# Edge lists of a graph layer: rows of keys gathered by their number, a written order on three engines, packed comparisons, norms loaded as rows

## The chip, the core and the metric

The kernel runs on one core of a Trainium2 chip. The metric is the device time of one execution in microseconds (us), lower being better; the time before is the median of three executions. One more execution was recorded by the hardware profiler, and all durations below come from it.

A core has TensorE (PE in the profile, with its weight loads as PEld), VectorE (DVE), ScalarE (ACT), GpSimd (POOL) and SyncE (SP). Each works through its own instructions in order. SP, ACT and POOL also issue transfers.

## What is computed

The input is a table x of 1250 rows of 768 numbers and an edge list of 41250 pairs (src, dst), sorted by dst. Reduced to what matters:

```python
def gat_layer(x, W, a_src, a_dst, b, src, dst):     # twice, relu between
    h = x @ W
    e = leaky_relu((h @ a_src)[src] + (h @ a_dst)[dst], 0.2)
    w = exp(e - segment_max(e, dst)[dst])
    alpha = w / segment_sum(w, dst)[dst]
    return segment_sum(h[src] * alpha[:, None], dst) + b

x = x + gat_layer(relu(gat_layer(layernorm(x), ...)), ...)
y = layernorm(x)
y = y + attention(layernorm(y, ln1_g, ln1_b))       # 12 heads of 64
y = y + moe(layernorm(y, ln2_g, ln2_b))             # 8 experts, the best 2 of each row
return x + y
```

Everything is float32.

## The kernel before

**The plan.** The 1250 nodes are ten tiles of 125 rows (T = 125, NT = 10). The graph layer isn't done edge by edge. The kernel first turns the edge list into a dense table `cnt`: how many edges lead from each source node to each target node. Then attention over edges is dense work on 1250 x 1250 tables, and the sum over edges is a matrix product with h. Everything up to the finished `cnt` is the first stage, and it is what the change is about. It ends near 144 us; the two graph layers, attention, routing and the experts follow.

**Keys and windows.** Each edge becomes a key, dst * 1250 + src. The keys, 330 to a row and 125 rows, lie in SBUF as `key` and are stored to DRAM as `keys`. For each node the kernel finds the position of its first edge, and a gather (an indirect DMA issued by GpSimd) fetches 64 keys from there: the node's window. To find the position, the kernel before makes a 0/1 table `within` (125 rows x 1250 nodes: does this node's first edge lie in this row?) from the first key of a row (`head`) and the first key of the next (`after`, from the small loads `rn`). For each tile, a matmul with `within` as weights fetches the one row of keys that belongs to each node (`pk`, L263), and VectorE counts the keys in it that are smaller than the node's own first possible key (L264) and adds the row's first edge number (L266). When all ten tiles are done, ten gathers follow (L275), and each window has the node's base subtracted (L305) to become `win`.

**Comparisons.** The windows, in which each entry is a source node's number or a mark for none, are transposed into `lt` and split into a tile number `jb` and a place within the tile `pb`. There are 625 pairs of nodes, taken in 25 groups of 25 (NP = 625, PG = 25). For each group VectorE compares pb with `lane` to make `oh` (L349, 128 x 128 x 25 in bfloat16); for every five groups it compares jb with `upto`, the numbers 1 to 20, to make `ohj` (L346). TensorE then takes one matmul for each pair (L353): oh's 128 columns as weights, 20 columns of ohj as the moving operand. ScalarE copies the counts into `cnt` (L357). `oh` has two buffers.

**Beside it.** The same stage normalises the ten tiles of x (statistics and `ln_stats` on VectorE, the root and the scaling on ScalarE at L123 and L298), transposes them into xnT (L136, copied out at L285), projects the first three tiles with W (L186, `EARLY` = 3), multiplies W by the two attention vectors (L169, `attention_vectors`; `rep` holds a vector copied to all partitions) and multiplies xnT by the results (L177, `attention_terms`, three chunks of six matmuls, copied out as `er`). A float32 matmul shows in the profile as two passes.

**Order.** A scheduler places the instructions on each engine. The programmer's order is one of its inputs and isn't kept. A loop over `turns` stands ready for lists that do not fit the windows; it makes no pass on these inputs. The four norm vectors, `lnp`, are loaded one number to a partition (L495), and the router's weights `wr` after them (L496); both are wanted only in the second graph layer and later, but the scheduler has put these loads at the beginning, on ACT's queue.

Of the kernel before, what the change touches and what calls it, by code (L numbers as in the profile page):

```python
# [10 lines left out]
F32 = mybir.dt.float32  # L11
F16 = mybir.dt.float16
BF16 = mybir.dt.bfloat16
# [14 lines left out]
def gnn_ffn_kernel(  # L28
# [24 lines left out]
    nc = tc.nc  # L53
# [62 lines left out]
    def ln_stats(row):  # L116
        st = small.tile([T, 2, 6], F32, tag="st", name="st")
        for s in range(2):
            nc.vector.bn_stats(st[:, s, :], row[:, s * DH:(s + 1) * DH])
        mv = small.tile([T, 2], F32, tag="mv", name="mv")  # L120
        nc.vector.bn_aggr(mv, st.rearrange("p a b -> p (a b)"))
        sd = small.tile([T, 1], F32, tag="sd", name="sd")
        nc.scalar.activation(sd, mv[:, 1:2], AF.Sqrt, bias=eps[:T])  # L123
        rstd = small.tile([T, 1], F32, tag="rstd", name="rstd")
        nc.vector.reciprocal(rstd, sd)
        return mv[:, 0:1], rstd
# [29 lines left out]
    with tc.tile_pool(name="cnt", bufs=1) as cpool:  # L156
# [6 lines left out]
        def attention_vectors(layer, w, a_src, a_dst, pool):  # L163
            for i, a in enumerate((a_src, a_dst)):
                rep = pool.tile([P, D], F32, tag="rep", name="rep", bufs=1)
                nc.scalar.dma_start(rep, bass.AP(tensor=a.tensor, offset=a.offset, ap=[[0, P], [1, D]]))
                for c in range(DC):
                    scr = pool.tile([P, D], F32, tag="scr", name="scr", bufs=1)
                    nc.vector.scalar_tensor_tensor(scr, w[:, c, :], 1.0, rep, op0=ALU.mult, op1=ALU.mult,  # L169
                                                   accum_out=wa[:, layer, c, i:i + 1])  # L170

        def attention_terms(layer, xT, psum):

            for c0, w in CHUNKS:
# [4 lines left out]
                nc.scalar.copy(er[:, c0:c0 + w], pe[0:2, :w])  # L179
# [16 lines left out]
        EARLY = 3  # L196
        with tc.tile_pool(name="edge", bufs=1) as ep, \
# [6 lines left out]
            rn = ep.tile([T, 2], I32, name="rn")  # L204
            nc.gpsimd.memset(rn, 2 * N)
            for i, (eng, a) in enumerate(((nc.sync, dst), (nc.scalar, src))):
                eng.dma_start(ri[:, i, :], a.rearrange("(p e) -> p e", p=T))
                with nc.allow_non_contiguous_dma(reason="one edge of each row"):
                    eng.dma_start(rn[0:T - 1, i:i + 1], a[EC:E].rearrange("(p e) -> p e", p=T - 1)[:, 0:1])
            xrows = []  # L210
            for t in range(4):
# [4 lines left out]
            rf = ep.tile([T, 2, EC], F32, name="rf")  # L216
            nc.vector.tensor_copy(rf, ri)
            key = ep.tile([T, EC + 1], F32, name="key")
            nc.vector.scalar_tensor_tensor(key[:, :EC], rf[:, 0, :], float(N), rf[:, 1, :],
                                           op0=ALU.mult, op1=ALU.add)  # L220
# [3 lines left out]
            nc.sync.dma_start(keys[0:E].rearrange("(p e) -> p e", p=T), key[:, :EC])  # L224
            nc.gpsimd.iota(key[:, EC:EC + 1], pattern=[[0, 1]], base=0, channel_multiplier=EC,
                           allow_small_or_imprecise_dtypes=True)
            after = ep.tile([T, 2], F32, name="after")
            nc.vector.tensor_copy(after, rn)
            nc.vector.scalar_tensor_tensor(after[:, 0:1], after[:, 0:1], float(N), after[:, 1:2],
                                           op0=ALU.mult, op1=ALU.add)  # L230
# [17 lines left out]
            upto = ep.tile([P, 2 * NT], BF16, name="upto")  # L248
            nc.gpsimd.iota(upto, pattern=[[1, 2 * NT]], base=1, channel_multiplier=0,
# [6 lines left out]
            within = ep.tile([T, N], F32, name="within")  # L256
            nc.vector.tensor_scalar(within, nodes, head, None, ALU.is_gt)
            nc.vector.scalar_tensor_tensor(within, nodes, after[:, 0:1], within, op0=ALU.is_le, op1=ALU.mult)
            junk = ep.tile([T, EC], F32, name="junk")
            place = ep.tile([T, NT], F32, name="place")  # L260
            for t in range(NT):
                pk = gpt.tile([P, 4, P], F32, tag="tr", name="pk").rearrange("p a b -> p (a b)")
                nc.tensor.matmul(pk[:T, :EC + 1], within[:, t * T:(t + 1) * T], key, start=True, stop=True)  # L263
                nc.vector.scalar_tensor_tensor(junk, pk[:T, :EC], node[:, t:t + 1], ones[:T, :],  # L264
                                               op0=ALU.is_lt, op1=ALU.mult, accum_out=place[:, t:t + 1])
                nc.vector.tensor_tensor(place[:, t:t + 1], place[:, t:t + 1], pk[:T, EC:EC + 1], ALU.add)  # L266
            nc.vector.tensor_scalar(place, place, 0.0, float(E), ALU.max, ALU.min)
            at = ep.tile([T, NT], I32, name="at0")
            begun = nc.vector.tensor_copy(at, place)

            win = ep.tile([T, NT, SL], F32, name="win")
            kws = []
            for t in range(NT):
                kw = op.tile([T, SL], F32, tag="kw", name="kw", bufs=NT)
                nc.gpsimd.indirect_dma_start(  # L275
                    out=kw, out_offset=None, in_=keys.rearrange("(e o) -> e o", o=1),
                    in_offset=bass.IndirectOffsetOnAxis(ap=at[:, t:t + 1], axis=0))
                kws.append(kw)
# [10 lines left out]
            for t in range(NT):  # L289
                if t < len(xrows):  # L290
                    xn = xrows[t]
                else:
                    xn = op.tile([T, D], F32, tag="xn", name="xn", bufs=4)
                    split_rows(nc.sync if t % 2 == 0 else nc.scalar, xn, x[t * T:(t + 1) * T, :])
                mean, rstd = ln_stats(xn)
# [711 lines left out]
```

## Time and profile before

| | |
|---|---|
| median of three executions | 1547.34 us (1546.9 to 1551.69) |
| the profiled execution | 1548.87 us; span from first to last instruction 1546.8 us |
| TensorE busy | 1458.0 us (94%), 5990 matmul passes |
| VectorE busy | 804.2 us (52%) |
| ScalarE busy | 597.5 us (39%) |
| GpSimd busy | 417.9 us (27%) |
| mean granted TensorE clock | 0.968 |
| first pass of L263, L353; last end of L353 | 22.27, 81.61 and 143.77 us |

A line of the order of time has the start, the length, the engine, the line of the kernel, the operation, what is written and read with its shape, how often, and in brackets how long the engine had been idle and what ended that. A line of a group has the number of instructions, then busy time in us and the mean in ns, then the idle time before them and its cause. A table by stretch has, for each engine, the busy time and the number of instructions, then the granted TensorE clock, the share of the DMA engines' time and GB/s.

### The profile page before, as it was taken

The numbers are of one execution on the slowest core, as the hardware profiler recorded it, in microseconds if no ns is written. First come the engines' busy times: TensorE is split into PE (matmuls) and PEld (weight loads), VectorE is DVE, ScalarE is ACT, GpSimd is POOL, SyncE is SP. The second block draws the span as 40 slices with busy tenths as digits, with TensorE's granted clock in tenths as the row PEclk, the third lists the DMA queues.
The fourth block names the chain that finished last, engine by engine and source line by source line (L and its number), as shares of the span: only waits on it lengthen the run. The fifth ranks groups of instructions, "written<-read, shape, count | busy, mean of one in ns | idle before, by whom it ended". The sixth has DMA issues, their size and how long they took to land.

```text
span 1546.8 us, 15957 instructions
## 1 busy us (share of the span) xinstructions
PE 1458.0 (94%) x5990; PEld 783.7 (51%) x5990; DVE 804.2 (52%) x1296; ACT 597.5 (39%) x949; POOL 417.9 (27%) x279
## 2 busy tenths in 40 slices
PE   4797999999999999999999999999988997899997
PEld 2466655554555555553434334334333565456664
DVE  5588643205315651016877877877889665111111
ACT  2422413202413631115665665665666354221211
POOL 3200000000000002004565565675676322122222
PEclk9975999999999999999999999999999998899999
DMA  5201020000021117951000000000030333854643
GB/s 148 56 1 34 8 72 0 1 2 9 0 72 53 57 50 278 406 196 61 1 21 1 22 0 21 1 21 1 1 100 1 111 120 124 302 167 171 229 143 139
DMA packets 50912, 123.83 MB, mean 80 GB/s; under 512 B 8542, under 2 KB 25045, under 8 KB 50833
## 3 DMA queue, kind: packets, MB, share of 16 engines
q1 hardware_dynamic: 30798, 55.21, 10.6%
q0 software_dynamic: 11408, 55.44, 9.5%
q10 hardware_dynamic: 8626, 12.15, 2.8%
q8 instruction: 48, 0.79, 0.2%
q14 instruction: 32, 0.25, 0.1%
HBM read 69.65 MB, written 57.60 MB: 82 GB/s over the span
## 4 chain that ended last, share of the span: by engine, by line
PE 65%; DVE 8%; issue 8%; DMA 4%; ACT 4%; POOL 1%; POOLq 0%; SPq 0%; DVEq 0%; ACTq 0%
PE pagg L465 12%; PE st L592 8%; PE ph L186 8%; PE pav L636 7%; PE pk L555 5%; PE pv L571 5%; PE phe L921 4%; PE pq L555 4%; PE poe L930 4%; DVE sT L622 2%; DMA xd<-yn,slot 2%; PE po L779 2%; ACT sT L595 1%; DMA out_dram<-sofar,ids 1%; DVE most L601 1%
## 5 line engine op out<-in xcount | busy, mean ns | idle before, releaser
L628 POOL TENSOR_TENSOR acc<-acc,sT 125x834 f32<-125x834 f32 (+1 forms) x139 | 272.9, 1963 | 10.9
L465 PE MATMUL pagg<-h,wt 125*125 125x385 f32 (+1 forms) x800 | 262.7, 486 | 0.4 <-DVE wt L458 0.4
L601 DVE TENSOR_TENSOR most<-most,st 125x834 f32<-125x834 f32 (+1 forms) x144 | 146.9, 1020 | 105.1 <-ACT sT L595 101.7
L465 PEld LDWEIGHTS pagg<-h,wt 125*125 125x125 f32 x800 | 147.4, 187 | 106.0 <-DVE wt L458 2.7
L622 DVE TENSOR_TENSOR sT<-sT,mb 125x834 f32<-125x834 f32 (+1 forms) x180 | 174.1, 1015 | 22.6 <-PE mb L617 22.6
L623 ACT ACTIVATE sT<-sT 125x834 f32<-125x834 f32 (+1 forms) x180 | 158.4, 900 | 49.2 <-DVE sT L622 48.9
L595 ACT COPY sT<-st 125x834 f32<-125x834 f32 (+1 forms) x180 | 151.5, 848 | 51.3 <-PE st L592 48.3
L592 PE MATMUL st<-qk 64*125 64x417 f32 (+1 forms) x720 | 164.6, 557 | 3.8 <-DVE most L601 3.8
L636 PE MATMUL pav<-sT,v 125*64 125x417 f32 (+1 forms) x720 | 150.8, 531 | 9.1 <-ACT sT L623 9.1
L533 POOL MEMSET zero<- 128x772 f32 x1 | 0.7, 741 | 538.9 <-PE ptr L136 538.9
L628 POOL TENSOR_TENSOR acc<-sT 125x834 f32<-125x834 f32 (+1 forms) x18 | 35.3, 1962 | 275.3 <-ACT sT L623 275.3
L592 PEld LDWEIGHTS st<-qk 64*125 64x125 f32 x720 | 56.6, 184 | 99.0 <-issue 42.7
L636 PEld LDWEIGHTS pav<-sT,v 125*64 125x64 f32 x720 | 42.5, 136 | 105.7 <-issue 43.9
L930 PE MATMUL poe<-we,hT 128*128 128x384 f32 x264 | 88.8, 486 | 0.0
L555 PE MATMUL pq<-yT,wqk 128*128 128x417 f32 (+1 forms) x216 | 88.1, 534 | 0.0
L779 PE MATMUL po<-wp,aT 128*125 128x384 f32 x240 | 87.5, 498 | 0.0
L921 PE MATMUL phe<-xT,we 128*128 128x384 f32 (+1 forms) x288 | 86.6, 460 | 0.0
L934 DVE SCALAR_TENSOR_TENSOR sofar<-poe,weight,sofar 128x768 f32<-128x768 f32 x25 | 25.4, 1018 | 115.2 <-PE poe L930 115.1
L555 PE MATMUL pk<-yT,wqk 128*128 128x417 f32 (+1 forms) x216 | 84.0, 526 | 0.0
L186 PE MATMUL ph<-gw,xnT 128*125 128x384 f32 x240 | 83.9, 505 | 0.0
L571 PE MATMUL pv<-wv,yT 128*125 128x384 f32 x240 | 79.9, 490 | 1.4 <-issue 1.4
L469 DVE RECIPROCAL rz<-pagg 125x1 f32<-125x1 f32 x20 | 3.3, 165 | 148.1 <-PE pagg L465 148.1
(218 smaller groups left out, 1807.7 us busy)
## 6 DMA issues: line engine op xcount, KB each, us to landing
xd<-zero POOLq DMA_DIRECT2D x8, 3860.0 KB
we<-in_L_ffn_W_dram SPq DMA_DIRECT2D x16, 1152.0 KB
xr<-xd SPq DMA_DIRECT2D x25, 386.0 KB
gw<-in_L_gnn_W_dram SPq DMA_DIRECT2D x2, 2304.0 KB
wqk<-in_L_ffn_Wqkv_dram SPq DMA_DIRECT2D x12, 384.0 KB
xres<-in_x_dram SPq DMA_DIRECT2D x10, 375.0 KB
xsd<-xres ACTq DMA_DIRECT2D x10, 375.0 KB
wv<-in_L_ffn_Wqkv_dram SPq DMA_DIRECT2D x1, 2304.0 KB
```

The source lines that it names most:

```text
L186: nc.tensor.matmul(po[:, s, :DH], xT[:, c, t * T:(t + 1) * T], w[:, c, s * DH:(s + 1) * DH], start=(c == 0), stop=(c == DC - 1))
L465: nc.tensor.matmul(po[:, s, :DH + s], ws[j][:, (d - d0) * T:(d - d0 + 1) * T], h[:, j, s * DH:(s + 1) * DH + s], start=(j == 0), stop=(j = ...
L555: nc.tensor.matmul(pq[:, :w], wqk[:, c, i, :], yT[:, c, c0:c0 + w], start=(c == 0), stop=(c == DC - 1))
L571: nc.tensor.matmul(pv[:T, s, :DH], yT[:, c, t * T:(t + 1) * T], wv[:, c, s * DH:(s + 1) * DH], start=(c == 0), stop=(c == DC - 1))
L592: nc.tensor.matmul(st[:T, i, :w], self.qk[r, 1, j * T:(j + 1) * T], self.qk[r, 0, self.c0:self.c0 + w], start=True, stop=True)
L595: nc.scalar.copy(s[:, :, :w], st[:T, :, :w])
L601: nc.vector.tensor_tensor(self.most[:, :, :w], prev[:, :, :w], st[:T, :, :w], ALU.max)
L622: nc.vector.tensor_tensor(s[:, :, :w], s[:, :, :w], self.mb[:T, :, :w], ALU.subtract)
L623: nc.scalar.activation(s[:, :, :w], s[:, :, :w], AF.Exp)
L628: nc.gpsimd.tensor_tensor(self.acc[:, :, :w], prev[:, :, :w], s[:, :, :w], ALU.add)
L636: nc.tensor.matmul(self.pav[r, :w], v[:, j, hd0:hd0 + HD], s[:, i, :w], start=(j == 0), stop=(j == NT - 1))
L930: nc.tensor.matmul(po[:, d, :DH], hT[:, f, s * P:(s + 1) * P], w2[:, f, d * DH:(d + 1) * DH], start=(f == 0), stop=(f == FC - 1))
```

## The change

In words, in the order of the diff:

- Finding a node's first edge: `begun`, one bfloat16 compare of `nodes` with `head`, replaces `within`; ten matmuls with a single column of ones count how many rows begin before each node, which gives the row's number; a gather by that number fetches the row of 330 keys from DRAM (`gather_row`, three buffers), and `first_edges` counts in it and issues the tile's window gather at once, straight into `win`. `rn` and `after` are gone. `keys` is stored from ACT's queue.
- A written order (`manual_schedule`) for TensorE, VectorE and GpSimd covers row numbers, statistics, normalisation, transposes, the three early projections, the attention vectors and twelve of the eighteen terms; a second one for TensorE and VectorE covers the comparisons, with one of the remaining six terms after every fourth group.
- `upto` and `ohj` are laid out so that the 125 pairs of five groups are innermost; `upto` is written out in full, and TensorE reads ohj's 20 columns 125 elements apart.
- The conversion of the edge lists to float32 (`rf`), which only the loop over `turns` reads, comes after the comparisons.
- The norm vectors are loaded as 24 rows of 128 numbers, transposed by TensorE and copied to `lnp`; these loads, `wr` and the attention vectors' loads keep their place in the program on ACT's queue.

The core of the diff:

```diff
-        def attention_vectors(layer, w, a_src, a_dst, pool):
+        def attention_vectors(layer, w, a_src, a_dst, pool, bufs):
+            def load(a):
+                rep = pool.tile([P, D], F32, tag="rep", name="rep", bufs=bufs)
+                tc.keep_in_program_order(nc.scalar.dma_start(rep, ...))
+                return rep
...
-                with nc.allow_non_contiguous_dma(reason="one edge of each row"):
-                    eng.dma_start(rn[0:T - 1, i:i + 1], a[EC:E].rearrange("(p e) -> p e", p=T - 1)[:, 0:1])
...
-            nc.vector.tensor_copy(rf, ri)
-            nc.vector.scalar_tensor_tensor(key[:, :EC], rf[:, 0, :], float(N), rf[:, 1, :], ...)
+            nc.vector.scalar_tensor_tensor(key, ri[:, 0, :], float(N), ri[:, 1, :], op0=ALU.mult, op1=ALU.add)
...
-            nc.sync.dma_start(keys[0:E].rearrange("(p e) -> p e", p=T), key[:, :EC])
+            nc.scalar.dma_start(keys[0:E].rearrange("(p e) -> p e", p=T), key)
...
-            upto = ep.tile([P, 2 * NT], BF16, name="upto")
-            nc.gpsimd.iota(upto, pattern=[[1, 2 * NT]], base=1, channel_multiplier=0,
+            upto = ep.tile([P, 2 * NT, 5 * PG], BF16, name="upto")
+            nc.gpsimd.iota(upto, pattern=[[1, 2 * NT], [0, 5 * PG]], base=1, channel_multiplier=0,
...
-            for t in range(NT):
-                pk = gpt.tile([P, 4, P], F32, tag="tr", name="pk").rearrange("p a b -> p (a b)")
-                nc.tensor.matmul(pk[:T, :EC + 1], within[:, t * T:(t + 1) * T], key, start=True, stop=True)
-                nc.vector.scalar_tensor_tensor(junk, pk[:T, :EC], node[:, t:t + 1], ones[:T, :],
-                                               op0=ALU.is_lt, op1=ALU.mult, accum_out=place[:, t:t + 1])
...
+            def find_rows():
+                nc.vector.tensor_scalar(begun, nodes, head, None, ALU.is_gt)
+                pk = epc.tile([P, 512], F32, tag="pc", name="pk")
+                for t in range(NT):
+                    nc.tensor.matmul(pk[:T, t:t + 1], begun[:, t * T:(t + 1) * T], oneb,
+                                     start=True, stop=True)
+                return pk
+            def gather_row(t):
+                krows[t] = op.tile([T, EC], F32, tag="kr", name="kr", bufs=LEAD)
+                nc.gpsimd.indirect_dma_start(
+                    out=krows[t], out_offset=None, in_=keys[0:E].rearrange("(p e) -> p e", p=T),
+                    in_offset=bass.IndirectOffsetOnAxis(ap=row[:, t:t + 1], axis=0))
+            def first_edges(t):
+                count = small.tile([T, 1], F32, tag="count", name="count")
+                nc.vector.scalar_tensor_tensor(key, krows[t], node[:, t:t + 1], ones[:T, :],
+                                               op0=ALU.is_lt, op1=ALU.mult, accum_out=count)
+                nc.vector.tensor_tensor(at[:, t:t + 1], count, edges[:, t:t + 1], ALU.add)
+                nc.gpsimd.indirect_dma_start(
+                    out=win[:, t, :], out_offset=None, in_=keys.rearrange("(e o) -> e o", o=1),
+                    in_offset=bass.IndirectOffsetOnAxis(ap=at[:, t:t + 1], axis=0))
...
+            def spread(t):
...
+                stats[t] = ln_root(xrows[t])
+            def normal(t):
+                mean, sd = stats.pop(t)
...
+                nc.scalar.activation(xrows[t], xrows[t], AF.Identity, scale=rstd, bias=less)
+            def columns(t):
+                transpose_rows(gpt, xrows[t], evict_to(xT, t))
...
+            with tc.manual_schedule(engines=fixed):
+                pk = find_rows()
+                spread(0)
+                nc.vector.tensor_scalar(row, pk[:T, :NT], -1.0, None, ALU.add)
+                nc.vector.tensor_scalar(edges, pk[:T, :NT], -1.0, float(EC), ALU.add, ALU.mult)
+                for t in range(LEAD):
+                    gather_row(t)
+                for t in range(4):
+                    if t > 0:
+                        spread(t)
+                        normal(t - 1)
+                normal(3)
+                for t in range(4):
+                    columns(t)
+                for t in range(NT):
+                    first_edges(t)
+                    if t + LEAD < NT:
+                        gather_row(t + LEAD)
+                    if t % 3 == 0 and t // 3 < EARLY:
+                        project(xT, gw, h, gpo, [t // 3])
+                    if 0 < t <= 6:
+                        spread(t + 3)
+                    vector(0 if t < 3 else 1 if t < 5 else 2)
+                    if 0 < t <= 6:
+                        normal(t + 3)
+                        columns(t + 3)
+                terms = attention_terms(0, xT, gpt)
+                for _ in range(2 * DC):
+                    next(terms)
+                nc.vector.tensor_tensor(win, win, node[:, :, None].to_broadcast([T, NT, SL]), ALU.subtract)
...
-                    nc.vector.tensor_tensor(ohj[:, js, :], jb[:, js, None].to_broadcast([P, 5 * PG, 2 * NT]),
-                                            upto[:, None, :].to_broadcast([P, 5 * PG, 2 * NT]), ALU.is_equal)
+            with tc.manual_schedule(engines={mybir.EngineType.PE, mybir.EngineType.DVE}):
+                for g in range(NP // PG):
+                    if g % 5 == 0:
+                        nc.vector.tensor_tensor(ohj[:, g // 5], jb[:, None, js].to_broadcast([P, 2 * NT, 5 * PG]), upto,
+                                                ALU.is_equal)
...
-                    nc.tensor.matmul(pc[:, k, :], oh[:, :, k], ohj[:, g * PG + k, :], start=True, stop=True)
+                        nc.tensor.matmul(pc[:, k, :], oh[:, :, k], ohj[:, g // 5, :, (g % 5) * PG + k], start=True, stop=True)
...
+                    if g % 4 == 3:
+                        next(terms, None)
...
+            nc.vector.tensor_copy(rf, ri)
...
-                nc.scalar.dma_start(lnp[:, i, :], a.rearrange("(c p) -> p c", p=P))
-            nc.scalar.dma_start(wr, Wrouter.rearrange("(c p) e -> p c e", p=P))
+                tc.keep_in_program_order(nc.scalar.dma_start(lnr[i * DC:(i + 1) * DC, :],
+                                                             a.rearrange("(c p) -> c p", p=P)))
+            tc.keep_in_program_order(nc.scalar.dma_start(wr, Wrouter.rearrange("(c p) e -> p c e", p=P)))
+            pt = gpt.tile([P, 4, P], F32, tag="tr", name="pln")
+            nc.tensor.transpose(pt[:, 0, :4 * DC], lnr, ident[:4 * DC, :4 * DC])
+            nc.scalar.copy(lnp.rearrange("p i c -> p (i c)"), pt[:, 0, :4 * DC])
```

## The prediction

> **What bounds the kernel now.** I read the slices first, then the order of time of each engine up to 150 us, then a table by stretch. The slices:
>
> ```profile
> PE   4797999999999999999999999999988997899997
> DVE  5588643205315651016877877877889665111111
> PEclk9975999999999999999999999999999998899999
> ```
>
> The PE row begins behind the label, each digit is 38.7 us. From 148 us on TensorE is nearly full; only the first four slices, where the edge lists become the count matrix, leave it idle, and there its granted clock drops. Everything the change moves ahead of 148 us lies there, so a gain is what those 144 us lose. Inside them, the order of time:
>
> ```profile
> 20.21 0.17 DVE L228 CAST after<-rn 125x2 f32<-125x2 int32 x1 [1.15 <-DMA rn<-in_dst_dram]
> 20.60 1.52 DVE L258 SCALAR_TENSOR_TENSOR within<-nodes,after,within 125x1250 f32<-125x1250 f32 x1
> 22.27 10.13 PE L263 MATMUL pk<-key,within 125*125 125x331 f32 x20 [22.27 <-DVE within L258]
> 33.94 1.79 POOL L275 DMA_INDIRECT kw<-keys,at  x1 [24.67 <-DVE at L269]
> 49.64 1.20 POOL L275 DMA_INDIRECT kw<-keys,at  x1 [0.30 <-issue]
> 54.15 0.25 DVE L305 TENSOR_SCALAR win<-kw,node 125x64 f32<-125x64 f32 x1 [0.70 <-DMA kw<-keys,at]
> 62.09 0.47 DVE L315 TENSOR_SCALAR win<-win 125x640 f32<-125x640 f32 x1
> 68.47 4.68 PE L186 MATMUL ph<-gw,xnT 128*125 128x384 f32 x14
> 72.99 0.28 PE L317 MATMUL psum<-found,ones 125*128 125x1 f32 x2
> ```
>
> Columns: start, length, engine, line. A 4-byte load (rn) queued behind the weights lands at 20.2; the fetch of key rows by TensorE takes until 32.4; ten gathers run from 33.94 to 50.84 (16.9 us, 1.69 each with the gap); the last lands 3.3 us later. The windows are ready at 62.6, but `psum` starts at 72.99, because projections stand ahead of it on TensorE. Then the comparisons, from 76.95 to 143.77:
>
> ```profile
> L349 DVE TENSOR_TENSOR ohp<-pb,lane 128x3200 bf16<-128x3200 bf16 x25 | 46.6, 1886 | 5.4 <-PE pc L353 4.4
> L353 PE MATMUL pc<-ohj,ohp 128*128 128x20 bf16 x625 | 45.5, 217 | 9.5 <-DVE ohp L349 9.3 <-DVEq L364 0.2
> L346 DVE TENSOR_TENSOR ohj<-jb,upto 128x2500 bf16<-128x2500 bf16 x5 | 13.7, 2748 | 0.0
> ```
>
> VectorE sets this stage (L349 25 x 1.89, L346 5 x 2.75); TensorE's group of 25 is close behind (1.84). The 4.4 us in which VectorE waits for TensorE is where matmuls of `attention_terms` stand between groups.
>
> **The change part by part, preamble.** I set two chains to `psum`.
>
> TensorE. The ten-fold fetch (10.13 us) becomes ten one-column matmuls: at the 1.84/25 = 0.074 of L353, 0.7 us, ready near 10.7. In their place the chain hangs on the keys' store. It moves from SP (issued 12.13, behind gw) to ACT, into the place of the first rep (issued 9.35), 0.80 to issue. Its landing is not shown. Lower end: 10.15 plus the 3.3 of a gather, 13.5. Upper end: the two edge-list loads of the same shape, issued near 0.8, first read at 7.79, so 6.5 after issue: 16.6. I take 16.0, near that row, since gw shares the engines. Three row gathers at 1.69: 21.1. As built, GpSimd's queue then has six small operations that before took 7.95 to 9.27 (1.3 us), and the fifth feeds VectorE's `before` operation, which stands ahead of the fourth tile's `normal`. That is the new wait: behind it are all first_edges. So normal(3) near 22.7, ACT 1.03, the fourth tile's transposes end at 24.7. Then in order: three projections at 24 passes x 0.3225 = 7.74 (30.96 for 96 at the L186 row of the chain), 23.2; six transposes of 0.81, 4.9; twelve terms at 7.16/10 = 0.716, 8.6; about 1.0 for tile 8, whose normalisation stands behind an h copy on ACT: 37.7. TensorE will have idled some 5 us before it; the trace shows what that costs:
>
> ```profile
> 48.03 1.50 PE L136 MATMUL ptr<-ident,xn 125*128 125x125 f32 x6 [5.12 <-ACT xn L298]
> 49.32 3.83 PE L186 MATMUL ph<-gw,xnT 128*125 128x384 f32 x8
> 48.00:53.00 5.00, 4.97 (x15) 3.33 (x16) 0.78 (x6) 2.33 (x5) 2.38 (x2) 0.66 0.60 177
> ```
>
> 1.50 against 0.81 and 3.83 against 2.58: 1.9 lost (clock 0.66). Sum: 24.7 + 37.7 + 1.9 = **64.3**.
>
> Gathers. Ten become twenty, in pairs of 2 x 1.69 = 3.4 us per tile: win(0) at 23.6, kr(3) lands 30.2, kr(9) at 50.5. VectorE's own work per step is 0.9 (L264, its accumulator, L266) + 1.2 (statistics) + up to 2.0 (two of L169) + 0.4, at most 4.5; statistics of tile 9 wait on ACT behind the second h copy (about 47.7), so first_edges(9) ends near 54.4, its gather lands at 59.3, and subtract, compare and pack (0.8 for the one subtract in place of ten of 0.25, then 0.47 + 0.90 + 0.77 + 0.47) end at 62.9. That is 1.4 under TensorE's 64.3, so ten added gathers cost nothing while TensorE covers them; without cover each costs 1.7. From psum's start to packed offsets stays as before, 72.99 to 77.0. Preamble: 72.99 - 64.3 = **8.7 saved**.
>
> **Comparisons.** L346 gets `upto` at full size, innermost step one on every side. Nearest row: L349, 3200 elements in 1.886; 2500 at that rate 1.47, I take 1.5: 5 x 1.25 = 6.2 saved. [...] all 25 of L349 lie between 1.875 and 1.894. I take the row.
>
> Order: the five waits (4.4) go. As built, twelve terms precede `psum` and six stand behind groups 3, 7, 11, 15, 19 and 23. What a term costs there depends on the clock:
>
> ```profile
> 74.52 7.16 PE L177 MATMUL pe<-xnT,wa 128*2 128x417 f32 x20 [0.66 <-ACT lt L331]
> 92.46 2.94 PE L177 MATMUL pe<-xnT,wa 128*2 128x416 f32 x4
> 76.90:97.90 21.00, 21.00 (x156) 10.79 (x154) 17.24 (x10) 4.21 (x12) 0.00 (x0) 0.92 0.01 2
> 97.90:143.80 45.90, 36.34 (x501) 34.87 (x500) 42.30 (x22) 12.79 (x40) 0.00 (x0) 0.52 0.00 1
> ```
>
> Two passes make a term: 0.72 at first, 1.47 at 92.46. [...] here TensorE was busy 36.34 of 45.90 us and was granted 0.52. [...] by the rows 1.47; I take 1.47. With two oh buffers, VectorE stalls 1.45 two groups after a term, unless an L346 operation lies between (3, 7, 19): twice 1.45, and behind group 23 the last group is 1.4 later: 4.3[...]. After: 25 x 1.907 (9.54 for five) + 7.5 + 2.9 + 1.9 + 1.4 = 61.4 against 66.8: **5.4 saved**.
>
> ohj is now read by TensorE with a step of 250 bytes. The trace has no such moving operand. Nearest: the weights of L353, 128 columns at a 50-byte step within 0.074, so 20 columns fit in 0.012 and hide: zero, and no reason for a gain. Upper end: as slow as fp32 columns at half clock, 1.47/2/417 = 1.8 ns, 20 of them 35 ns unhidden.
>
> **At zero.** `upto` on GpSimd grows from 20 to 2500 elements: 4.81 x 2500/3200 = 3.8, to about 11.6, under the keys' landing at 16; uncovered, 3.8. The rf cast (0.56) lies beside the last group. Removed norm loads (ACT's queue, 13.8 to 20.9) free that queue; their rows come after layer 1, where the one transpose costs TensorE 0.3 and ACT's es copy comes some 4 us later, under 57 us of L186 from 384; uncovered, 4. The second layer's vector loads keep their neighbours on ACT and wait for gw2 until 217 anyway. SP loses one store and rn; its tile loads now follow gw directly.
>
> Sum: 8.7 + 5.4 - 0.3 = **13.8**. The profiled execution has a span of 1546.8 and 1548.87 in all, 1.5 above the median 1547.34. Predicted median 1547.34 - 13.8 = **1533.5**.
>
> **Rivals.** (a) Better, 0.22: the keys land at 13.5 and the clock holds: TensorE's chain gives 59.9, the gathers' 60.4, so 3.9 more there and 2.3 on the terms, 20 saved, 1527. For: nothing but gw contends; against: the clock rows. (b) Gathers bind, 0.14: a row gather is 1.3 KB against 256 B, so 2.3 each instead of 1.69: twenty add 12 to 62.9, psum near 74, the preamble saves nothing, 5 left, 1542.5. For: the row's spread of 1.18 to 1.82; against: its mean. (c) Slower, 0.07: the strided ohj. TensorE becomes the bound of the comparisons when a group passes 1.907; with six terms (8.8) and the head (3.4), the whole gain is gone when 25 groups take 66.8 + 8.4 - 12.2 = 63, 2.5 a group, 101 ns per pair instead of 74. At the upper end, 109 ns, 68: 5 slower, 1552. For: TensorE is only 0.07 below VectorE; against: the weights' row. (d) The lists don't all fit the windows and the loop over `turns` runs: it doesn't run before and the windows stay 64 wide; under 0.01.
>
> **How the numbers follow.** The main case has 0.56, own range 1529 to 1539. With (a) and (b) it takes 0.92; range 1522 to 1543. What a measurement can tell from no change is 0.3%, 4.6 us: part of (b) falls inside. Faster 0.87, same 0.06, slower 0.07.
>
> **What would show it.** Right: no pk fetch; twenty DMA_INDIRECT ending near 56; VectorE waiting for GpSimd ahead of the fourth normal; psum near 64; L346's successor near 1.5; VectorE stalls of 1.4 near groups 13 and 17; the last pc near 129.5; from there on everything equal. Wrong: VectorE waiting for gathers up to psum (b), groups of pc above 1.9 (c), or a compare still at 2.75.

## The result and the profile after

Six executions of the kernel after have a median of 1541.69 us (1540.3 to 1542.49), six of the kernel before on the same chip 1547.63 (1546.86 to 1551.69): a ratio of 0.9955, 95% interval 0.9941 to 0.9968. The kernel is faster, by about 6 us. On a second chip it was 1539.16 against 1548.36, ratio 0.9939 (0.9924 to 0.9954), 9 us. The forecast was 1533.5, a gain of 13.8.

The profiled execution took 1542.12 us, its span 1540.3 (before 1546.8). The slices, again 38.5 us to a digit:

```profile
PE   3889999999999999999999999999988997799998
DVE  4698633205326740117877877877888665011111
PEclk9956999999999999999999999999999997899999
```

Behind the fourth digit the PE row is that of before but for single tenths. The first digit is even lower than before (3 for 4), and the clock in the third is lower (5 for 7).

Names used from here on: `psum` is the matmul that counts the edges found in the windows, the first of TensorE's instructions that needs them all (through `found`); `pl` are the transposes of `win` behind it, and `pec` is the first matmul of the graph layer behind the comparisons. spread(t) and normal(t) are the statistics and the normalisation of tile t, columns(t) its transposes, project(n) one of the three early projections. They count from 0: the fourth tile is tile 3.

The order of time up to `psum` (start, length, engine, line, operation, idle time before it and what ended that; the first line is the issue of the keys' store):

```profile
9.81 0.26 ACTq L233 DMA_DIRECT2D keys<-key  x1
20.41 1.38 POOL L278 DMA_INDIRECT kr<-keys,row  x1 [10.18 <-issue]
25.83 0.23 DVE L812 TENSOR_SCALAR before<-before 125x125 f32<-125x125 f32 x1 [9.16 <-POOL before L810]
26.36 1.03 ACT L319 ACTIVATE xn<-xn,less,rstd 125x768 f32<-125x768 f32 x1 [8.56 <-DVE less L318]
27.80 3.79 PE L140 MATMUL ptr<-ident,xn 125*128 125x125 f32 x15 [10.16 <-ACT xnT L298]
31.38 8.88 PE L201 MATMUL ph<-gw,xnT 128*125 128x384 f32 x24
60.74 1.65 POOL L288 DMA_INDIRECT win<-keys,at  x1 [0.92 <-DVE at L287]
63.02 8.56 PE L190 MATMUL pe<-xnT,wa 128*2 128x417 f32 x24 [0.62 <-ACT xnT L298]
67.33 0.49 DVE L370 TENSOR_SCALAR win<-win 125x640 f32<-125x640 f32 x1
71.52 0.38 PE L372 MATMUL psum<-found,ones 125*128 125x1 f32 x2
```

The fetch of key rows is gone from TensorE, but TensorE stands still from 17.6 to 27.8. Read upwards: it waits for ScalarE's copies, ScalarE for `less` of the fourth tile, VectorE for the routing table `before`, and GpSimd makes that table only after three row gathers, the first of which starts at 20.41, 10.6 us after the issue of the keys' store that it reads. The windows are ready at 67.8, and `psum` follows at 71.52 when TensorE has done its terms: only 1.5 us earlier than before. The groups of the comparisons, 75 to 140 us (count, busy time, mean ns, idle before):

```profile
L405 DVE TENSOR_TENSOR ohp<-pb,lane 128x3200 bf16<-128x3200 bf16 x25 | 46.5, 1885 | 3.8 <-PE pc L409 3.0
L409 PE MATMUL pc<-ohj,ohp 128*128 128x20 bf16 x625 | 45.3, 221 | 9.4 <-DVE ohp L405 9.2
...
L402 DVE TENSOR_TENSOR ohj<-jb,upto 128x2500 bf16<-128x2500 bf16 x5 | 7.3, 1460 | 0.0
```

`ohj` halved, 2748 to 1460 ns. From packed offsets (75.98) to the last group's end (136.03) it is 60.05 us, against 66.8 before.

The balance of the profiles: 1.5 at `psum`, less 0.5 (psum to packed offsets took 4.46, before 3.96), plus 6.75 in the comparisons make 7.7 us at the first `pec` of the graph layer (138.2 for 145.9), where the stage is over. From `pec` to the end of the span it is 1402.1 us after and 1400.9 before. In the twelve runs below that rest takes 1400.2 to 1403.8, whatever was edited. The 1.2 between before and after lies inside that spread: neither a loss behind the stage nor an effect of the norms' loads shows, and up to 3.6 us of a difference of medians can lie in the rest. The experiments are therefore read at `psum` and `pec` of the profiles, with the medians beside them.

### The profile page after: what moved, and what is told of

Its sections match the earlier page's. It is cut to its first block, busy times and chain, and to the rows that moved or that the text cites. A ratio compares the mean times of both kernels' runs of the same rounds, so it can differ in the third digit from the quotient of the medians.

```text
span 1540.3 us, 15938 instructions
## 1 busy us (share of the span) xinstructions
PE 1454.5 (94%) x5981; PEld 782.3 (51%) x5981; DVE 797.8 (52%) x1285; ACT 597.6 (39%) x950; POOL 431.6 (28%) x287
## 4 chain that ended last, share of the span: by engine, by line
PE 71%; DVE 9%; issue 8%; DMA 5%; ACT 4%; POOL 2%; POOLq 0%; SPq 0%; ACTq 0%; DVEq 0%
PE pagg L525 12%; PE ph L201 9%; PE st L659 8%; PE pav L703 7%; PE pk L622 5%; PE pv L638 5%; PE phe L988 5%; PE poe L997 5%; PE pq L622 4%; DMA xd<-yn,slot 2%; DVE sT L689 2%; PE pc L409 2%; PE pe L190 2%; PE po L846 2%; PE ptr L140 1%
## 5 line engine op out<-in xcount | busy, mean ns | idle before, releaser
L689 DVE TENSOR_TENSOR sT<-sT,mb 125x834 f32<-125x834 f32 (+1 forms) x180 | 174.1, 1016 | 22.9 <-PE mb L684 22.9
L201 PE MATMUL ph<-gw,x1T 128*125 128x384 f32 x240 | 78.6, 487 | 0.0
```

What stands on the lines that cost most here:

```text
L201: nc.tensor.matmul(po[:, s, :DH], xT[:, c, t * T:(t + 1) * T], w[:, c, s * DH:(s + 1) * DH], start=(c == 0), stop=(c == DC - 1))
L689: nc.vector.tensor_tensor(s[:, :, :w], s[:, :, :w], self.mb[:T, :, :w], ALU.subtract)
```

## The experiments

Theory: the 7.2 us that the preamble lacks against the forecast (71.5 for 64.3) went into waits that start at the keys' landing. Rivals: the gathers, GpSimd or the transfer of `rep` set the pace; or what the first stage gains is given back later. Runs 1 to 4 shared one chip, 5 to 8 a second, 9 to 11 a third, and 12 had a fourth; each chip has its own runs of the kernel before (medians 1547.39, 1548.36, 1548.07 and 1548.81), to which the ratios refer.

| run | first row gather | project(0) | psum | pec | median (executions) | ratio to before |
|---|---|---|---|---|---|---|
| after | 20.4 | 31.4 | 71.5 | 138.2 | 1541.69 (6) | 0.9955 (0.9941 to 0.9968) |
| 1 table first | 19.4 | 22.9 | 68.5 | 135.1 | 1540.70 (7) | 0.9958 (0.9943 to 0.9974) |
| 2 keys in two stores | 16.5 | 27.5 | 67.0 | 133.7 | 1537.51 (6) | 0.9939 (0.9922 to 0.9957) |
| 3 old ohj | 20.5 | 31.5 | 71.5 | 144.4 | 1547.82 (14) | 0.9994 (0.9983 to 1.0005) |
| 4 = 1, gw behind keys | 15.8 | 23.0 | 68.6 | 135.2 | 1535.86 (6) | 0.9920 (0.9899 to 0.9940) |
| 5 = 1, rep early | 19.6 | 23.0 | 68.9 | 135.5 | 1540.14 (5) | 0.9943 (0.9930 to 0.9956) |
| 6 = 5, two stores | 18.1 | 22.8 | 67.2 | 133.9 | 1537.32 (6) | 0.9930 (0.9914 to 0.9947) |
| 7 = 6, six terms behind pl | 16.8 | 23.0 | 64.1 | 130.8 | 1532.61 (4) | 0.9894 (0.9880 to 0.9908) |
| 8 after again | 21.5 | 32.4 | 72.5 | 139.1 | 1539.16 (6) | 0.9939 (0.9924 to 0.9954) |
| 9 = 5, new order | 20.0 | 22.9 | 65.1 | 131.7 | 1535.71 (5) | 0.9925 (0.9912 to 0.9939) |
| 10 = 7, new order | 17.4 | 23.0 | 62.9 | 130.4 | 1532.54 (4) | 0.9899 (0.9883 to 0.9914) |
| 11 = 10, twelve terms behind pl | 16.3 | 23.0 | 59.5 | 125.7 | 1530.99 (5) | 0.9904 (0.9889 to 0.9920) |
| 12 = 11, keys first | 13.8 | 22.9 | 63.6 | 129.8 | 1531.60 (4) | 0.9888 (0.9872 to 0.9905) |

**Run 1: the table `before` at the program's start.**

```diff
 nc.gpsimd.iota(iota8, ...)
+before = gate.tile([T, T], F32, name="before")
+nc.gpsimd.iota(before, pattern=[[1, T]], base=0, channel_multiplier=-1, ...)
+nc.vector.tensor_scalar(before, before, 0.0, None, ALU.is_gt)
...
-(the same three, ahead of the routing)
```

> The kernel after, but the routing table's iota and comparison (the tile before, 125x125) stand at the program's start, ahead of lane, instead of behind the first three row gathers; nothing else moves. Theory A: VectorE's 9.16 us wait for that tile held the fourth tile's normalisation, ScalarE's copies behind it and so TensorE from 17.6 to 27.8 us. Then the fourth tile is scaled at about 17 us, its columns end at about 21, project(0) starts there, as gw is in (the DMA engines' traffic falls off at about 19.5), and psum comes at 60 to 64 us instead of 71.5: the median falls by 7 to 11 us, to 1531 to 1535. Theory B: the keys' landing at 20.4 and the gathers behind it bind as soon as TensorE is freed (after had win ready at 67.8, 3.7 us ahead of psum): the median falls by at most 3.7 us, to 1538 to 1541.7. Theory C: the wait is of no consequence: within 1 us of 1541.7.

The order of time of run 1:

```profile
22.88 9.40 PE L201 MATMUL ph<-gw,xnT 128*125 128x384 f32 x24
24.79 0.56 DVE L285 SCALAR_TENSOR_TENSOR key<-kr,node,ones 125x330 f32<-125x330 f32 x1 [7.35 <-DMA kr<-keys,row]
29.87 0.29 ACT L123 ACTIVATE sd<-mv,eps 125x1 f32<-125x1 f32 x1 [6.27 <-DVE mv L121]
36.66 1.51 PE L140 MATMUL ptr<-ident,xn 125*128 125x125 f32 x6 [3.75 <-ACT xnT L298]
37.97 8.68 PE L201 MATMUL ph<-gw,xnT 128*125 128x384 f32 x24
40.45 0.96 DVE L181 SCALAR_TENSOR_TENSOR scr<-gw,rep 128x768 f32<-128x768 f32 x1 [5.46 <-DMA rep<-in_L_gnn_att_src_dram]
68.49 0.38 PE L372 MATMUL psum<-found,ones 125*128 125x1 f32 x2
```

The wait is gone and project(0) starts 8.5 us earlier, as theory A said, but `psum` gains 3.0, inside B's limit, and the median only 1. The wait had sat in front of others: VectorE now stands at `first_edges` for the first row of keys, the fifth tile's statistics stand behind that, ScalarE stands 6.27 us for them, TensorE 3.75 for ScalarE.

**Run 2: the keys stored as 112 and 13 rows.**

```diff
-nc.scalar.dma_start(keys[0:E].rearrange("(p e) -> p e", p=T), key)
+split_rows(nc.scalar, keys[0:E].rearrange("(p e) -> p e", p=T), key)
```

> The kernel after, with the keys' store issued as 112 and 13 rows instead of 125 rows at once; one issue of about 0.3 us more on ScalarE's queue. The keys landed at 20.4 us, 10.6 us after their issue at 9.8, for 161 KB. If the shape of the store [...] is the cause, the first row gather starts at 14 to 17 us and the comparison of the tile before follows at 19 to 22, so the median falls by 3 to 6 us, to 1536 to 1539. If the cause is that the store shares the engines with gw's 2.3 MB, issued 0.3 us before it, the first gather stays at 19.5 to 20.7 and the median within 1 us of 1541.7.

The order of time of run 2:

```profile
16.50 1.38 POOL L278 DMA_INDIRECT kr<-keys,row  x1 [6.26 <-DVE rstd L316]
21.93 0.23 DVE L812 TENSOR_SCALAR before<-before 125x125 f32<-125x125 f32 x1 [5.24 <-POOL before L810]
27.47 8.30 PE L201 MATMUL ph<-gw,xnT 128*125 128x384 f32 x24
67.03 0.38 PE L372 MATMUL psum<-found,ones 125*128 125x1 f32 x2
```

The first gather starts 3.9 us earlier, VectorE's table 3.9, project(0) 3.9, `psum` 4.5, the median 4.2: the keys' landing passes through to `psum` one to one, with every wait behind it left in place. The shape of the store is a cause of it: from issue to first gather it is 10.6 us with 125 rows at once and 6.8 with 112 and 13. Why is not shown.

**Run 3: `ohj` in the old layout.**

```diff
+up1 = ep.tile([P, 2 * NT], BF16, name="up1")          # filled by an iota, 1 to 20
-ohj = ep.tile([P, NP // (5 * PG), 2 * NT, 5 * PG], BF16, name="ohj")
+ohj = ep.tile([P, NP, 2 * NT], BF16, name="ohj")
-nc.vector.tensor_tensor(ohj[:, g // 5], jb[:, None, js].to_broadcast(...), upto, ALU.is_equal)
+nc.vector.tensor_tensor(ohj[:, js, :], jb[:, js, None].to_broadcast(...), up1[:, None, :].to_broadcast(...), ...)
```

> The kernel after, with the five offset comparisons in the layout of the kernel before (element by element over edges and values, the table up1 of 20 values beside the wide one, which stays so that the start of the program is the same). Theory: each takes 3.1 us instead of 1.47, VectorE sets the pace between groups, and the part from packed offsets to the last group is 66 to 67 us instead of 60.05. If the gain of that part comes through to the end whole, the median rises by 6 to 7 us, to 1548, that of the kernel before. Rival: what is saved in the first 140 us is partly given back at the end of the program, where the profile after has 29.64 us of waiting for the scatter of rows against 26.54 before: then the median rises by only 3 to 5 us, to 1545 to 1547.

The group in run 3:

```profile
L402 DVE TENSOR_TENSOR ohj<-jb,up 128x2500 bf16<-128x2500 bf16 x5 | 13.8, 2751 | 0.0
```

Each comparison took 2.75 us, as in the same layout before (2748 ns), and not the 3.1 of my estimate. `psum` as after, `pec` 6.2 us later, median 6.1 higher: the kernel before's time, with a ratio of 0.9994. (The 1.5 us by which `pec` is still ahead of before, 144.4 for 145.9, lie inside the spread of the rest.) So the packed comparison carries the whole gain that the median shows, and nothing of it is given back at the end.

**Run 4: run 1 with gw loaded behind the keys, on ScalarE's queue.**

```diff
-gw = load_big_weight(gW1, "gw1")                      # on SP, ahead of the keys
...
 nc.scalar.dma_start(keys[0:E]..., key)
+gw = wpool.tile([P, DC, D], F32, tag="w", name="gw1")
+tc.keep_in_program_order(nc.scalar.dma_start(gw, ...))
```

> The kernel of the first run (the tile before at the program's start), and gw's load issued on ScalarE's queue right behind the keys' store instead of on SP's at 9.5 us. If sharing the DMA engines with gw is why the keys took 10.6 us to land, the first row gather now starts at 12.5 to 15 us, and gw is in some 1 to 3 us later than the 19.5 of the first run. What follows depends on which binds then: if the gathers bind in the first run, this one is 2 to 5 us faster than it; if gw and TensorE bind there, it is 0 to 3 us slower. If gw is not the cause, the first gather stays at about 20 us and the two are within 1.5 us of each other.

gw ahead of the keys is a cause as well: with gw issued 0.3 us behind them it is 5.7 us from issue to first gather, against 9.7 in run 1. gw isn't missed, project(0) starts at 23.0. But the first row of keys is read at 23.52, only 1.3 us earlier than in run 1: 7.8 us behind the start of its gather, 5.4 there. That gw, now later, held the row up is my estimate and not shown. VectorE waits 5.56 us for `rep` at 38.2. `psum` and `pec` are those of run 1. The median is 4.8 lower than run 1's, of which the stage that was edited shows nothing; 2.9 of it lie between the rests of the two profiles, 1403.8 and 1400.9. I don't count it.

**Run 5: run 1 with `rep` loaded early, on SP behind gw.**

```diff
 key = ep.tile([T, EC], F32, name="key")
+reps = [op.tile([P, D], F32, tag="rep", name="rep", bufs=2) for _ in range(2)]
+[nc.sync.dma_start(r, ...) for r, a in zip(reps, (ga_src1, ga_dst1))]
```

> The kernel of the first run (the tile before at the program's start), with the two replicated attention vectors (rep) loaded on SP's queue right behind gw instead of on ScalarE's behind the seventh tile's standard deviation. In the first run project(0) started 8.5 us earlier than after (22.9 instead of 31.4), yet psum only 3.0 earlier (68.5), and VectorE waited 5.46 us for rep at 35 to 40 us. Theory A1: rep is the wait that took the place of the one removed; without it psum comes at 63 to 65.5 and the median falls by 3 to 5 us against the first run. Rival: what holds the order there is the keys' landing alone, since the fifth tile's statistics stand on VectorE behind the first edges of two columns (ScalarE waited 6.27 us for them): then psum stays above 67 and the two are within 1.5 us.

The order of time of run 5:

```profile
26.25 0.56 DVE L285 SCALAR_TENSOR_TENSOR key<-kr,node,ones 125x330 f32<-125x330 f32 x1 [8.72 <-DMA kr<-keys,row]
29.16 1.02 DVE L119 BATCH_NORM_STATS2 st<-xn 125x6 f32<-125x384 f32 x2
35.78 0.30 ACT L123 ACTIVATE sd<-mv,eps 125x1 f32<-125x1 f32 x1 [1.00 <-DVE mv L121]
35.98 0.78 ACT L204 COPY h<-ph 125x768 f32<-125x768 f32 x1
37.19 1.51 PE L140 MATMUL ptr<-ident,xn 125*128 125x125 f32 x6 [4.07 <-ACT xnT L298]
68.86 0.38 PE L372 MATMUL psum<-found,ones 125*128 125x1 f32 x2
```

My theory A1 falls: no wait for `rep` any more, and `psum` is 0.4 later than in run 1. The lines show the path: the row of keys at 26.25, then tile 4's statistics, and so on to the seventh tile's root at 35.78; ScalarE's copy of project(0)'s result, done on TensorE at 30.9, stands behind that root, and the copies of xnT stand behind it.

**Run 6: runs 1, 2 and 5 together.**

> The three together: before at the program's start, the keys' store in 112 and 13 rows, rep loaded early. If the preamble's missing 7 us were these three waits, TensorE goes on from the fourth tile's columns at about 23 us with some 40 us of its own work, and psum comes at 61 to 64 us (71.5 after, 64.3 in the forecast); the median is 7 to 10 us below after's, 1531.5 to 1534.5. If the gathers bind once the rest is out of the way, twenty at 1.5 us from 16.5 on and 5.4 us behind the last one, win is ready at 55 to 60 and they still do not bind; if VectorE's forty-odd small operations pace them as in the second run (last gather at 57, win about 62), psum comes at 62 to 64, the same to the eye, but TensorE is then seen waiting for found at psum.

`psum` at 67.2, no better than run 2 alone, and not the 61 to 64 that I expected: project(1)'s transposes waited 3.81 us at 35.2, and project(1) took 9.60 instead of 7.91. Win was subtracted at 55.75, so it did not bind.

**Run 7: run 6 with six of the terms moved behind the transposes of `win`.**

```diff
-for _ in range(2 * DC):
+for _ in range(DC):
     next(terms)
...
 with tc.manual_schedule(engines={PE, DVE}):
+    for _ in range(DC): next(terms)
     for g in range(NP // PG):
```

> The kernel of the three together, with six of the twelve terms that stand ahead of psum moved behind the transposes of win (pl), where TensorE had 6.42 us of waiting for the first comparison. If TensorE's order sets psum, it comes 4.3 us earlier (half of the 8.56 us of terms) and the six terms behind pl fit in the 6.42 us: the median falls by 3.5 to 4.5 us against the kernel of the three. If win is only just in time there, psum waits for found and the fall is 0 to 2 us.

The order of time of run 7, TensorE:

```profile
64.12 0.38 PE L372 MATMUL psum<-found,ones 125*128 125x1 f32 x2
...
66.06 4.36 PE L190 MATMUL pe<-xnT,wa 128*2 128x417 f32 x12 [0.54 <-ACT lt L386]
71.95 3.64 PE L409 MATMUL pc<-ohj,ohp 128*128 128x20 bf16 x50 [1.52 <-DVE ohp L405]
```

`psum` 3.1 earlier, `pec` 3.1, the median 4.7. It is not the 4.3 expected at `psum`, as the passes ahead of the terms took longer and the terms began 1.1 later than in run 6 (59.83 for 58.72). TensorE's order set `psum`, and the moved terms lie in its wait for the first comparison, which shrinks from 6.42 us to 1.52.

**Run 8: the kernel after again.**

> The kernel after once more, on this chip, so that it stands beside the others: 1540.5 to 1542.5 us by both theories. Its profile shows how much of a difference of 1 or 2 us lies in the end of the program: from the last rank product (prk) to the end of the span the kernel before took 236.6 us, after 237.4, and the four experiments 237.1 to 238.9.

The median is 1.3 us under the expected band. The profile differs from the first by 1 us throughout, from the keys' store (10.38 for 9.81) to `pec`, and its rest is 1400.5.

**Run 9: run 5 with another order.**

```diff
 for t in range(NT):
+    if t < 6: spread(t + 4); normal(t + 4)
     first_edges(t)
...
-    if 0 < t <= 6:
-        spread(t + 3)
     vector(...)
     if 0 < t <= 6:
-        normal(t + 3)
         columns(t + 3)
```

> The kernel of the fifth run (before at the program's start, rep loaded early, the keys' store unsplit), with one change of order in the hand-written part: the statistics and the normalisation of tile t+4 stand ahead of first_edges(t) instead of those of tile t+3 behind it. In the fifth and sixth runs taking waits away one by one left psum at 67 to 69 us: VectorE met the same late row of keys at its next instruction, the fifth tile's statistics stood behind it, ScalarE's copies behind those, and columns(5) on TensorE behind them (4.07 us of waiting at 37.2, and project(1) 8.67 instead of 7.91 after it). Theory A3: it is VectorE's order that hands the keys' lateness on to TensorE. Then, with the keys as late as in the fifth run, TensorE's wait at columns(5) is gone and psum comes at 62 to 64.5 instead of 68.9; the median falls by 4 to 7 us against the fifth run, to 1533 to 1536. Rival: TensorE is held by the gathers themselves or by ScalarE's own load, whatever VectorE's order: psum stays above 67 and the two are within 1.5 us.

The order of time of run 9:

```profile
23.03 1.02 DVE L119 BATCH_NORM_STATS2 st<-xn 125x6 f32<-125x384 f32 x2 [5.58 <-DMA xn<-in_x_dram]
26.29 0.56 DVE L285 SCALAR_TENSOR_TENSOR key<-kr,node,ones 125x330 f32<-125x330 f32 x1 [1.28 <-DMA xn<-in_x_dram]
33.98 1.17 PE L140 MATMUL ptr<-ident,xn 125*128 125x125 f32 x6 [1.87 <-ACT xnT L298]
65.11 0.38 PE L372 MATMUL psum<-found,ones 125*128 125x1 f32 x2
```

The keys are as late as ever (20.0, read at 26.29), and `psum` comes 3.8 us earlier, the median 4.4. The lateness reached TensorE through the order on VectorE. It was 0.6 short of the expected 64.5, since 1.87 of the wait at columns(5) is left: VectorE now waits for the fifth tile of x.

**Runs 10 and 11: run 7 with this order; then all twelve remaining terms behind `pl`.**

> The seventh run's kernel (before at the start, keys in two stores, rep early, six terms behind pl) with the order of the run ahead of this one. TensorE's wait of 3.46 us at columns(5) and the 2 us that project(1) was longer behind it go; psum at 58.5 to 61 instead of 64.1, where it begins to meet win (VectorE's subtraction was at 55.9 in the seventh run and found about 3.5 us later). The median falls by 3 to 5.5 us against the seventh run, to 1527 to 1530. If win is held by VectorE's own work, which now has the later tiles ahead of the edges, psum waits for found and the fall is 0 to 2 us.

> The kernel ahead of this one, with the last six terms too behind pl, so that none stands between the groups of comparisons: 12 terms of 0.71 us, 8.6 us, in TensorE's wait of 6.4 us, instead of six of 0.71 and six of 1.55 between the groups. TensorE has 9.3 us less between the groups, VectorE's 25 comparisons of 1.885 and 5 of 1.46 (54.4 us) then set the pace; after had 56.7 us from the first group to the last and two waits of 1.3 us of TensorE for VectorE. Expected: the part from pl to the last group 1 to 3 us shorter. If the comparisons are VectorE's alone already, 0 to 1 us; if the 2.2 us by which the terms overrun the wait are paid in full, 0 to 1 us slower.

Run 10 missed: `psum` 62.9 and the same median as run 7. columns(5) still waited 2.98 us and project(1) took 8.78. At `psum` TensorE waits for `found`, with 0.17 us, and VectorE was the later of the two: win was subtracted at 60.57 instead of 55.94. Run 11 has the best `pec`, 4.7 ahead of run 10. Of that, 3.4 were at `psum`, ahead of everything that the edit moves: the fifth tile of x landed at 21.94 instead of 24.00, and win was subtracted at 57.11. (The profiled execution was also the fastest of its five, 1529.12.) The other 1.3 is the edit's, within the expected 1 to 3; the median fell by 1.5. TensorE in run 11:

```profile
62.16 8.55 PE L190 MATMUL pe<-xnT,wa 128*2 128x417 f32 x24 [0.53 <-ACT lt L386]
...
81.48 3.64 PE L409 MATMUL pc<-ohj,ohp 128*128 128x20 bf16 x50 [1.32 <-DVE ohp L405]
```

The terms run over: TensorE starts the first group at 70.64 without a wait, and stands 0.31 us for VectorE ahead of the third, at 74.48. Behind that the 1.32 recurs at each `ohj`: the rest of the stage is VectorE's alone.

**Run 12: run 11 with the keys ahead of gw and `rep`** (both loads on ScalarE's queue behind the two stores).

> The kernel ahead of this one, with gw and rep loaded on ScalarE's queue behind the keys' two stores, so that the keys go ahead of everything but the first four tiles of x. Two questions. What the keys' landing consists of: the two stores alone gave a first gather at 16.5 us, gw behind the keys alone one at 15.8, and 20.4 without either. If shape and sharing are two causes that add up, it is now at 12.5 to 14 us; if each is only a way of getting ahead of gw's traffic, it stays at 15 to 16.5. And what it is worth now: in the kernel ahead of this one win's subtraction came at 57.1 us and psum at 59.5, set by TensorE and win together. If win is 2 to 4 us earlier and gw is not missed by project(0) at 23 us, psum comes at 57 to 59.5 and the median is 0 to 2.5 us lower, at 1528.5 to 1531. If gw, now behind, holds project(0), the median is 1 to 4 us higher.

The order of time of run 12:

```profile
13.81 1.38 POOL L278 DMA_INDIRECT kr<-keys,row  x1 [3.39 <-DVE st L119]
27.04 1.02 DVE L119 BATCH_NORM_STATS2 st<-xn 125x6 f32<-125x384 f32 x2 [9.52 <-DMA xn<-in_x_dram]
36.40 1.50 PE L140 MATMUL ptr<-ident,xn 125*128 125x125 f32 x6 [4.97 <-ACT xnT L298]
```

Shape and gw's place each count beside the other: 4.4 us from issue (9.40) to first gather, against 6.8 with the two stores alone (run 2) and 5.7 with gw alone moved (run 4). They do not add up in full (10.6 less 3.8 and less 4.9 would be 1.9). It bought nothing: gw isn't missed (project(0) starts at 22.9), but the fifth tile of x, at the head of VectorE's order, now lands at 27.0 (21.94 in run 11), and `psum` is 4.1 later than in run 11. Runs 7, 10, 11 and 12 all lie 15 to 17 us under before and can't be ranked by their medians.

## Why the prediction was wrong in size

- **What bounds: right.** The gain came from the first 144 us alone. The windows were ready 3.7 us ahead of `psum`; TensorE's order set it.
- **The keys' landing: the term that failed.** "I take 16.0", between 13.5 and 16.6; it was 20.4, outside the bounds. The upper bound came from the edge lists' loads, which run with no gw beside them. Run 2 gives 16.5 with another shape, run 4 15.8 with gw behind the keys, run 12 13.8 with both. That row held for this shape with no gw ahead of it (run 4: 5.7 us from issue to first gather, where the row gave 6.5); this shape behind gw, 10.6, is what no row had. Those 4.4 us moved the fourth `normal` to 26.0 instead of 22.7; part was made up because a gather's pitch was 1.5, not 1.69.
- **The new wait: right in its place, and mis-sized behind it.** VectorE waited for GpSimd's table ahead of the fourth `normal`, as forecast. But "the fourth tile's transposes end at 24.7" left only that tile to do, 2.0 us after `normal`. ScalarE's copies of the three tiles before stood behind the same scaling, so fifteen transposes followed, ending at 31.4: 5.4 us after `normal`. That is the other 3.4. Run 2 bears the split out: with the keys there at 16.5, near the forecast, `psum` came at 67.0, so 4.5 of the 7.2 hang on the landing and 2.7 are left.
- **From there to `psum`: right, 40.1 for 39.6, but in part by luck**: it held only because the wait had let the rest catch up. Take it away (run 1) and the same chain takes 45.6: the keys are still late, and VectorE's written order hands that on at its next instruction. The forecast priced one wait; what it had was a late arrival in front of a fixed order, with several instructions that would meet it.
- **Gathers: right that they don't bind** (rival b is out): 1.2 us and a gap of 0.3 for a row of 1.3 KB as for a window, where rival b supposed 2.3, so no dearer on GpSimd (to the landing it was 4.3 against 3.4, medians). They ended at 62.4, not 56, since VectorE fed them late.
- **Comparisons: right, 60.05 for 61.4.** All five `ohj` took 1.46 to 1.47 against 1.5. A term between groups took 1.55, at a granted clock of 0.50 with TensorE busy 36.5 of 39.0 us (97 to 136 us): the row held. VectorE stalled 1.37 and 1.36 us ahead of groups 14 and 18, as forecast near 13 and 17. TensorE's groups stayed at 1.85, so rival c is out. Run 3 shows that this part is the gain.
- **At zero: nothing against it.** With the norms' loads changed, the rest behind `pec` stays inside its spread.

Preamble 8.7 forecast and 1.5 found; comparisons 5.4 and 6.75, less 0.5 between them. No rival fits; it is the main case with 7 us lost to the landing and to what stood behind it. Why the rest behind `pec` varies by 3.6 us stays open.

## What to carry to other kernels

Bound the landing of a small transfer on which a stage hangs by a row with the same traffic beside it, and look at its shape and at what was issued just ahead of it: here 3.8 and 4.9 us of 10.6 hung on these two. In the written order here, removing one wait on a late arrival only showed the next instruction that met it (run 1: 8.5 us at project(0), 3.0 at `psum`; run 5: nothing at `psum`): list all that stand behind it on each engine, and either bring the arrival forward (run 2: 4.5 us at `psum`) or move what doesn't need it ahead (run 9: 3.8). Where two chains meet, work that neither needs yet can go into the gap behind the meeting point (run 7: 3.1).

## What the runs showed of the hardware

A store of 161 KB took 10.6 us from issue to the first gather that reads it, with 2.3 MB of weights issued 0.3 us ahead on another queue; 6.8 in two pieces, 5.7 with the weights behind it, 4.4 with both. It recurs: 9.7 to 11.1 us in five profiles with one store behind the weights (after and runs 1, 5, 8 and 9), 6.7 to 7.5 in the five with two (runs 2, 6, 7, 10 and 11). In the profile after, the store stood on ACT's queue and the weights on SP's: its 10.6 us show that the other queue did not shield it. From 10 to 20 us the 16 DMA engines were busy 0.85 of the time on average in that profile, and 0.95 before.

Two operations of VectorE took longer beside GpSimd's writing of `upto`. The order of time, first one line of the kernel before, then the kernel after, both engines:

```profile
13.03 0.15 DVE L240 TENSOR_SCALAR node<-node 125x10 f32<-125x10 f32 x1
...
7.69 2.51 POOL L252 IOTA upto<- 128x2500 bf16 x1
8.29 1.98 DVE L243 TENSOR_SCALAR node<-node 125x10 f32<-125x10 f32 x1
8.47 2.45 DVE L269 TENSOR_SCALAR begun<-nodes,head 125x1250 bf16<-125x1250 f32 x1
```

Ten numbers to a row took 1.98 us (0.15 before the change, with GpSimd idle), and both operations ended within 0.8 us of the iota's end at 10.20. In run 1 the iota ended at 10.42 and `begun` at 11.09. Not every operation was held: `key`, from 7.55 on, took 0.50 and `head`, at 8.09, 0.15, as before the change. What made the difference is not shown. It cost nothing here: `begun` ended at 10.92, and the first gather started at 20.41.

project(1), 24 passes, was slower behind some of TensorE's waits. It took 7.91 us where TensorE had waited 0.62 to 2.06 us just ahead of it (after and runs 2, 3, 8 and 11), at a granted clock of 1.00 in the profile after. In runs 1, 5, 6, 7, 9, 10 and 12, with waits of 1.87 to 4.97 us, it took 8.67 to 9.96. The length of the wait does not settle it alone: run 9 had its loss (9.38) after 1.87 us, run 11 had none after 2.06. Nor is it shown that a lower clock was the cause: before, a wait of 5.12 us stood beside a granted clock of 0.66 (48 to 53 us), but after, project(0) took 8.88 us behind a wait of 10.16 and fifteen transposes with 1.00 in the row throughout. In the runs project(0) took 7.91 us (5, 6, 8 and 12) to 9.40 (1); why stays open.

TensorE's busy time alone did not hold the clock up. Before, TensorE was busy in the whole of every microsecond from 75 to 100 us, and the granted clock was 1.00 up to 92, 0.50 from 93 to 95, 1.00 from 96 to 99 and 0.50 from 100 to 143.8. In the profile after it went from 1.00 to 0.50 between 74 and 75 us, while TensorE stood still, and was 0.50 from 79.34 to 100 us, with TensorE busy for 20.22 of 20.66 us. What decides is not shown here.
